# A join of two transfer chains in a Mamba and MoE kernel: queued with both chains as inputs, its gate released by its due landing

## The chip, the core and the metric

The program runs on one core of one Trainium2 chip. The metric is the device time of one execution in microseconds; the runs given are medians of several executions. A core has five queues that run in order by themselves and wait for each other through semaphores: PE (TensorE, matrix products into the PSUM banks), DVE (VectorE), ACT (ScalarE), POOL (GpSimd) and SP (SyncE, which here only issues transfers). POOL also issues transfers that add to what already lies at their target. An instruction that waits holds everything behind it in its own queue.

## The reference: what is computed

A "macaron" layer on 4 x 1024 tokens of 128 features: half a mixture of experts, a Mamba block, half a mixture of experts again, each with a layer norm in front and a residual around it.

```python
x = x + 0.5 * ffn(layernorm(x), ...)
x = x + attn(layernorm(x), ...)          # the Mamba block
x = x + 0.5 * ffn(layernorm(x), ...)

# ffn: 8 experts, every expert on every token, weighted
h = silu(x @ w_gate[e]) * (x @ w_up[e]); out += cw[e] * (h @ w_down[e])
# cw: product of two softmaxes over the experts (one at temperature 0.1), made to sum to one

# attn (Mamba, d_inner 256, 16 states)
xs, z = split(x @ W_in);  xc = silu(conv4(xs) + conv_b)
dbl = xc @ W_x;  dt = softplus(dbl[:, :64] @ W_dt + b_dt);  B, C = dbl[:, 64:80], dbl[:, 80:96]
h[t, :, n] = exp(dt * A[:, n]) * h[t-1, :, n] + dt * xc * B[t, n]
y[t] = sum over n of h[t, :, n] * C[t, n]  +  xc * D
out = (y * silu(z)) @ W_out
```

The sum over the 16 states n is the part that this change touches.

## The kernel before

**Tiling and stages.** The 4096 tokens are 8 blocks of 512. Each block goes through three stages: first mixture (kind 1), Mamba (m0 to m7), second mixture (kind 2). The 16 mixture stages run one after the other and make up the main loop; `order` lists them: kind 1 for blocks 0 to 3, then both kinds in turn. A mixture stage is 16 "halves" of two 128-wide slices each: six products into the PSUM tile `pg` (`gate_part`), a Silu on ACT into `h` (L536), six products into `pu` (`up_part`), `h * pu` on DVE (L561), and the down products of an earlier half into `pd` (L614). `pg` and `pu` have one buffer each, so the `pu` products of a half can't start before the L561 of the half before has read `pu`. On the finished `pd` of an expert ACT copies it to `tmp` (L636), and POOL multiplies it by the expert's weights and adds it to `acc` (L645, L648).

**The Mamba work rides along.** While one block's mixture runs on PE, the Mamba stage of another is fed in between as events. A block's 16 states take, per state n: `exp(dt*A)` on ACT (L892), on DVE the product with B (L906, `prod`), two scans (L918, `step`) and the product with C, either on DVE (L964) or "aside" on POOL (L954). The result of state n then has to be summed. `gather` does that by adding transfers that POOL issues: even n into `y`, odd n into the tile of state 1, called `odd`; so there are two chains, (k, 0) and (k, 1), each in order within itself. After state 15 a last transfer, the **join** (L938), adds `odd` to `y`. Then the **gate** multiplies `y` by silu(z): on DVE in blocks 0 and 7 (L986, `quick`), on POOL in the others (L991). Then PE does the output projection (`outproj`, tile `po`, L1002) and DVE adds it to x (L1009).

**Who sets the order.** The schedule is written out by hand: the order of the calls is the order of the instructions of each queue. A planner, `Plan`, keeps a modelled clock for each engine (`plan.pe`, `plan.dve`, `plan.act`, `plan.pool`), adds the cost given to each piece of work, and puts off work whose inputs aren't due. `plan.hi` and `plan.lo` hold pending DVE work; `lo` holds the states' products and scans. `fill` puts them into DVE's queue while they fit by the model before the next L561.

POOL has its own list, `pend`. `pool_put` appends an item: [function, cost, ready time, done, due time, chain, lane]. If `plan.lo` is empty it runs the whole list at once; otherwise items are run after each state's `prod` (`pool_run`) or by `pool_flush`. `pool_next` takes, of the first item of each chain, the one that can start earliest; `pool_start` gives that time: the ready time, `plan.pool`, and for a transfer the landing of the chain's last transfer, which its lane holds. A transfer is modelled to land YDMA = 5.9 after its issue.

**The join and gate before.** `gather` puts the join into chain (k, 0) with a ready time of the later of its data and the odd lane's landing, plus YDMA. When the join is run, its function first runs what is left of chain (k, 1) (L936, L937). The gate is an event of the list `back` at slot EPI + v + GT; its condition holds as soon as the join has been put into the list, that is once `scanned` exists. The gate then calls `pool_need`, which runs chain (k, 0) up to and with the join. Events that are held are forced after 12 slots (WAIT).

**Other work named later.** `dtfin` makes `dx` for the next Mamba block, on POOL (L881) in blocks 1 to 7; its states' first product L906 needs it. `cw1` to `cw3` make a mixture's weights by turns on POOL (L448, L454, L460) and DVE (L446, L453, L459); `cwt` transposes them on PE (L469). `zproj` (L975) makes z. The PSUM bank `misc` is shared by all the small products, among them `zproj`, `cwt` and `outproj`.

Of the kernel before, what the change touches and what calls it, by code (L numbers as in the profile page):

```python
# [25 lines left out]
EPI = 130  # L26
# [6 lines left out]
GT = 4  # L33
# [12 lines left out]
NEVER = 1e9  # L46
WAIT = 12
LOAD = 3.0
YDMA = 5.9
# [124 lines left out]
def tile_macaron_mamba_moe(  # L174
# [25 lines left out]
    NS = A_log.shape[1]  # L200
# [379 lines left out]
    def down(s, c):  # L580
# [41 lines left out]
        def weigh():  # L622
            cwb = d.pop(("cwb", e))
            d["tail"] = True
            plan.dve = max(plan.dve, pool_need(d["sum"]))
            tmp = sb.tile([P, TB], F32, tag="tmp", bufs=TMP, name=f"tmp_{kind}_{k}_{e}")
            V.tensor_tensor(tmp, pd, cwb, ALU.mult)
            V.tensor_tensor(d["acc"], d["acc"], tmp, ALU.add)
            plan.dve += 0.6
# [38 lines left out]
    def ffn_end(s):  # L668
        kind, k = order[s]
        d = ffn.pop(s)  # L670
        if "take" in d:
            plan.act_need(d["take"])
        plan.need(lambda: not d.get("tmp") or d["tmp"][3])
        at = d["tmp"][4] if "tmp" in d else pool_need(d["sum"])
        pt = misc(f"fo_{kind}_{k}")
        for j in range(J):
            T.transpose(pt[:, j * P : (j + 1) * P], d["acc"][:, j * P : (j + 1) * P], ident)
        x = xt[k]

        def upd():  # L680
            V.tensor_tensor(x, x, pt.rearrange("p (j h) -> p j h", j=J), ALU.add)
            fed.add(k)
            if kind == 2:
                nc.sync.dma_start(
                    out=of[k * TB : (k + 1) * TB, :].rearrange("(j p) h -> p j h", p=P), in_=x
                )

        plan.reader = plan.put(upd, 0.6, plan.on_pe(0.44, at))
# [15 lines left out]
    pend, credit = [], [0.0]  # L704

    def pool_put(fn, cost, ready, chain="w", dma=None):
        it = [fn, cost, ready, False, None, chain, dma]
        pend.append(it)
        if not plan.lo:
            pool_run(None)  # L710
        return it

    def pool_start(it):
        at = max(it[2], plan.pool)
        if it[6] is not None:
            at = max(at, it[6].get("landed", 0.0))
        return at

    def pool_next():
        heads, seen = [], set()  # L720
        for it in pend:
            if it[5] not in seen:
                seen.add(it[5])
                heads.append(it)
        return min(heads, key=pool_start) if heads else None

    def pool_run(after):
        credit[0] = min(credit[0] + CAP, CAP)
        while pend and (after is None or credit[0] > 0.0):
            it = pool_next()  # L730
            if after is not None and it[6] is not None and pool_start(it) > max(plan.pool, plan.dve) + AHEAD:
                break
            pool_one(after, it)

    def pool_one(after, it):
        pend.remove(it)
        ins = it[0]()
        it[3] = True
        if it[6] is not None:
            plan.pool = pool_start(it) + it[1]  # L740
            it[4] = it[6]["landed"] = plan.pool - it[1] + YDMA
            return
        credit[0] -= it[1]
        it[4] = plan.on_pool(it[1], max(it[2], plan.dve))
        if after is not None:
            tc.add_manual_dep(
                ins.ins, after.ins.name, mybir.DependencyInfo(mybir.DependencyClass.Sync, mybir.DependencyReason.DATA),
                reason="shared SBUF port",
            )

    def pool_flush():
        while pend:
            it = pool_next()
            if it[6] is None or pool_start(it) > max(plan.pool, plan.pe - 1.0):
                return
            pool_one(None, it)

    def pool_need(it):
        if it not in pend:
            plan.need(lambda: it[3])  # L760
        while not it[3]:
            pool_one(None, next(o for o in pend if o[5] == it[5]))
        return it[4]


    def mamba_events(k):
        d = {}
# [120 lines left out]
        def exps(n):  # L888
            plan.need_lo(4 * OUT)
            da = d["da", n] = big(f"da_{nm}_{n}")  # L890
            for i in range(ND):
                S.activation(da[:, i, :], d["dt"][:, i, :], AF.Exp, scale=A_sb[:, i, n : n + 1])  # L892
            t = plan.on_act(1.22, 0.0, "exp")
            if n == 0:
                if fast:
                    plan.need(lambda: d["dx_it"][3])
                else:
                    t = max(t, pool_need(d["dx_it"]))
            for f, cost in ((prod, 1.21), (lambda n: step(n, 0), 1.2), (lambda n: step(n, 1), 1.2), (read, 1.2)):
                it = plan.put(lambda f=f: f(n), cost, t, low=True)  # L900
            d["read", n] = it
# [21 lines left out]
        lane = [{}, {}]  # L923

        def gather(n, da, at):
            q = n % 2
            if n == 1:
                d["odd"] = da
            else:
                to = d["odd"] if q else d["y"]  # L930
                it = pool_put(lambda: G.dma_start(out=to, in_=da, accum_op=ALU.add), 0.9, at, (k, q), lane[q])
            if n < NS - 1:
                return

            def join():
                while any(o[5] == (k, 1) for o in pend):  # L936
                    pool_one(None, next(o for o in pend if o[5] == (k, 1)))  # L937
                return G.dma_start(out=d["y"], in_=d.pop("odd"), accum_op=ALU.add)  # L938

            ready = max(at, lane[1].get("landed", 0.0)) + YDMA  # L940
            d["scanned"] = pool_put(join, 0.9, ready, (k, 0), lane[0])

        def read(n):
            hb = d.pop("hb")
            da = d.pop(("da", n))
            bcb = d.pop(("bcb", n))
            d.pop(("read", n))
            plan.act_need(*d["y_it"])
            if d["aside"]:
                if not last:  # L950
                    V.tensor_reduce(st_sb[:, :, n : n + 1], da[:, :, TB - 1 : TB], AX.X, ALU.max)

                def weigh():
                    ins = G.tensor_tensor(da, da, bcb[:, 1:2, :].to_broadcast([P, ND, TB]), ALU.mult)  # L954
                    ahead["free"] += 1
                    pump()
                    return ins

                pool_put(weigh, 2.4, plan.dve, (k, n % 2))
                gather(n, da, plan.dve + 2.5)  # L960
                return
            if not last:
                V.tensor_copy(st_sb[:, :, n : n + 1], hb[:, :, TB - 1 : TB])
            V.tensor_tensor(da, hb, bcb[:, 1:2, :].to_broadcast([P, ND, TB]), ALU.mult)  # L964
            ahead["free"] += 1
            pump()
            gather(n, da, plan.dve + 0.1)

        def zproj(i):
                if i == 0:  # L970
                    d["zs"] = big(f"zs_{nm}")
                zs = d["zs"]
                d["zp"] = i + 1
                pz = misc(f"z{i}_{nm}")
                T.matmul(pz, w_in_sb[:, DI + i * P : DI + (i + 1) * P], d["xT"], start=True, stop=True)  # L975
                S.activation(zs[:, i, :], pz, AF.Silu)
                plan.bank = plan.on_act(0.6, plan.on_pe(0.86), "silu")
# [41 lines left out]
        v = w + LATE[k]  # L1019
# [31 lines left out]
        for q in range(NS // 2):  # L1051
# [8 lines left out]
        back = [  # L1060
            (EPI + v, lambda: zproj(0), free),
            (EPI + v + 2, lambda: zproj(1), free),
            (EPI + v + GT, gate, lambda: 0.0 if "scanned" in d else NEVER),
            (EPI + v + PO + (0 if quick else POW), outproj, lambda: max(free(), gated_at())),
        ]

        def gated_at():
            return (d["gated"][4] if d["gated"][3] else NEVER) if "gated" in d else NEVER
# [3 lines left out]
    chains = []  # L1072
# [19 lines left out]
    for s in range(len(order)):  # L1092
        add(8 * GPS * s, ffn_events(s))
        kind, k = order[s]
# [3 lines left out]
    for k in range(NBLK):  # L1098
        front, mid, back = mamba_events(k)
        add(START[k], front)  # L1100
        add(START[k], mid, 99)
        add(START[k], back)
# [62 lines left out]
```

## Time and profile before

| what | value |
|---|---|
| three runs | 1292.55, 1292.98, 1295.13 us; median 1292.98 |
| the profiled execution, its own time | 1294.15 us |
| its span, first to last instruction | 1292.4 us |
| matmuls on PE, DVE, ACT, POOL instructions | 4728, 1253, 1171, 624 |
| adding transfers from POOL into `y` and into `odd` | 72 and 56, 512 KB each |
| median from issue to landing of these | 9.1 and 9.5 us |
| the join, issue to landing, least, median, largest of 8 | 4.4, 4.5, 5.3 us |
| mean granted TensorE clock | 0.997 |

A line of a timeline reads: start in us, duration in us, engine, source line, operation, output<-inputs, how many were merged, and in brackets the idle time of that engine just before and what ended it. A line of the table of waits reads: engine, tile and line that waited, what it waited for, total us, times, longest us. A line of the table by stretches gives, for a stretch of time, the busy time of each engine with its number of instructions, the granted TensorE clock as a share of full speed, and the load of the transfers. Where the releaser is named "issue" the profile shows nothing that was waited for; a wait for several things is put down to the last that the profile saw, which can name the wrong one.

### The profile page before, as it was taken

Reading aid. Unit: us, or ns where it says so; the run is one execution under the profiler, and the core shown is the slowest. Engines: PE = TensorE matmul, PEld = TensorE weight load, DVE = VectorE, ACT = ScalarE, POOL = GpSimd, SP = SyncE. Lnnn points to the kernel's source line nnn. Section 1 sums busy time; section 2 is a strip of 40 time slices with the busy share of each in tenths; the row PEclk is TensorE's granted clock in tenths of the full one; section 3 lists DMA queues with packets and bytes.
Section 4 is the critical chain, followed back from the end, with each engine's and each line's share of the span. In section 5 each row is a group of like instructions: output and inputs, shape, how many; then the busy total and the mean of one; then the engine's idle time right before and its main releaser. Section 6 shows DMA issues by size and latency. Waiting matters only on the chain.

```text
span 1292.4 us, 14294 instructions
## 1 busy us (share of the span) xinstructions
PE 1257.2 (97%) x4728; PEld 853.9 (66%) x4728; DVE 1050.8 (81%) x1253; ACT 901.5 (70%) x1171; POOL 660.3 (51%) x624
## 2 busy tenths in 40 slices
PE   7999999989999999999999999999999999999998
PEld 5776665656666666666666666666666666668885
DVE  5875599978895899889769998997698889957675
ACT  5775766857867769767667786676777787646663
POOL 1012364637565647575467576554566657543400
PEclk9999999999999999999999999999999999999999
DMA  3420368757675668786737787676377867751110
GB/s 120 140 64 25 84 165 193 172 149 159 135 178 143 163 152 173 173 178 157 187 89 184 164 203 177 142 190 143 82 176 156 208 144 183 184 116 49 33 35 24
DMA packets 90635, 180.65 MB, mean 140 GB/s; under 512 B 9408, under 2 KB 22592, under 8 KB 90560
## 3 DMA queue, kind: packets, MB, share of 16 engines
q1 hardware_dynamic: 72128, 112.61, 31.8%
q0 software_dynamic: 18432, 67.12, 26.5%
q8 instruction: 37, 0.61, 0.2%
q14 instruction: 38, 0.31, 0.1%
HBM read 109.71 MB, written 2.88 MB: 87 GB/s over the span
## 4 chain that ended last, share of the span: by engine, by line
PE 73%; DMA 6%; DVE 4%; ACT 4%; issue 3%; POOL 3%; SPq 0%; POOLq 0%; DVEq 0%; ACTq 0%
PE pd L614 21%; PE pu L545 7%; PE pg L545 7%; PE pu L547 7%; PE pu L546 7%; PE pg L547 7%; PE pg L546 7%; DMA bcb_m<-bc_m 3%; PE pd L600 2%; DMA da_m<-da_m 2%; PE pd L608 1%; DMA y_m<-da_m 1%; DVE h L561 1%; PE xs_m L798 1%; ACT da_m L892 1%
## 5 line engine op out<-in xcount | busy, mean ns | idle before, releaser
L561 DVE TENSOR_TENSOR h<-h,pu 128x1024 f32<-128x1024 f32 x256 | 311.1, 1215 | 176.0 <-PE pu L547 124.4
L614 PE MATMUL pd<-h,wd 128*128 128x512 f32 x848 | 403.7, 592 | 1.4 <-ACT acc L636 0.7
L536 ACT ACTIVATE h<-pg 128x1024 f32<-128x1024 f32 x256 | 262.5, 1026 | 160.1 <-PE pg L547 156.5
L545 PE MATMUL pg<-xh_f,wh 128*128 128x512 f32 x512 | 272.5, 532 | 2.3 <-ACT h L536 1.4
L645 POOL TENSOR_TENSOR tmp<-tmp,cwb 128x512 f32<-128x512 f32 x98 | 137.1, 1399 | 208.6 <-ACT tmp L636 76.6
L614 PEld LDWEIGHTS pd<-h,wd 128*128 128x128 f32 x848 | 158.0, 189 | 114.3 <-issue 93.4
L545 PE MATMUL pu<-xh_f,wh 128*128 128x512 f32 x512 | 211.7, 414 | 3.1 <-DVE h L561 2.9
L547 PE MATMUL pg<-xh_f,wl 128*128 128x512 f32 x512 | 202.7, 396 | 0.0
L546 PE MATMUL pu<-xl_f,wh 128*128 128x512 f32 x512 | 202.4, 395 | 0.0
L546 PE MATMUL pg<-xl_f,wh 128*128 128x512 f32 x512 | 202.3, 395 | 0.0
L547 PE MATMUL pu<-xh_f,wl 128*128 128x512 f32 x512 | 202.1, 395 | 0.0
L954 POOL TENSOR_TENSOR da_m<-da_m,bcb_m 128x1024 f32<-128x1024 f32 x67 | 161.5, 2411 | 47.0 <-DVE hb_m L906 47.0
L906 DVE TENSOR_TENSOR hb_m<-dx_m,bcb_m 128x1024 f32<-128x1024 f32 x128 | 169.9, 1327 | 11.1 <-DMA bcb_m<-bc_m 8.1
L892 ACT ACTIVATE da_m<-dt_m,A_sb 128x512 f32<-128x512 f32 x256 | 163.9, 711 | 0.6
L545 PEld LDWEIGHTS pg<-xh_f,wh 128*128 128x128 f32 x512 | 96.7, 189 | 68.6 <-issue 30.9
L648 POOL TENSOR_TENSOR acc<-acc,tmp 128x512 f32<-128x512 f32 x98 | 137.1, 1399 | 7.7
L546 PEld LDWEIGHTS pg<-xl_f,wh 128*128 128x128 f32 x512 | 97.1, 190 | 52.3 <-issue 38.7
L545 PEld LDWEIGHTS pu<-xh_f,wh 128*128 128x128 f32 x512 | 96.7, 189 | 32.7 <-DVE h L561 7.6
L546 PEld LDWEIGHTS pu<-xl_f,wh 128*128 128x128 f32 x512 | 96.7, 189 | 24.8 <-issue 4.1
L547 PEld LDWEIGHTS pu<-xh_f,wl 128*128 128x128 f32 x512 | 96.7, 189 | 22.6
L547 PEld LDWEIGHTS pg<-xh_f,wl 128*128 128x128 f32 x512 | 96.5, 189 | 22.6
L636 ACT COPY tmp<-pd 128x512 f32<-128x512 f32 x111 | 64.7, 583 | 66.6 <-PE pd L614 55.1
(137 smaller groups left out, 1649.1 us busy)
## 6 DMA issues: line engine op xcount, KB each, us to landing
bcb_m<-bc_m SPq DMA_DIRECT2D x128, 512.0 KB
y_m<-da_m POOLq DMA_DIRECT2D x72, 512.0 KB, 9.1
cwb<-cd_f SPq DMA_DIRECT2D x128, 256.0 KB
da_m<-da_m POOLq DMA_DIRECT2D x56, 512.0 KB, 9.5
x<-in_L_attn_x_dram SPq DMA_DIRECT2D x8, 256.0 KB
wraw<-in_L_ffn_w_gate_dram SPq DMA_DIRECT2D x8, 256.0 KB
wraw<-in_L_ffn_w_up_dram SPq DMA_DIRECT2D x8, 256.0 KB
wd<-in_L_ffn_w_down_dram SPq DMA_DIRECT2D x8, 256.0 KB
```

Of the source, the lines that this page charges most:

```text
L536: S.activation(h, pg, AF.Silu)
L545: T.matmul(o[:, q, :], wh[e][:, i, cols], d["xh"], start=True, stop=False)
L546: T.matmul(o[:, q, :], wh[e][:, i, cols], d["xl"], start=False, stop=False)
L547: T.matmul(o[:, q, :], wl[e][:, i, cols], d["xh"], start=False, stop=True)
L561: V.tensor_tensor(h, h, pu, ALU.mult)
L614: T.matmul(d["pd"], wd[e][:, cols], h[0], start=(f == 0), stop=(f == FC - 1))
L636: S.copy(t, pd)
L645: it = put(lambda: G_.tensor_tensor(t, t, cwb, ALU.mult), 1.25, at)
L648: it = put(lambda: G_.tensor_tensor(acc, acc, t, ALU.add), 1.25, at)
L892: S.activation(da[:, i, :], d["dt"][:, i, :], AF.Exp, scale=A_sb[:, i, n : n + 1])
L906: mul = V.tensor_tensor(hb, d["dx"], bcb[:, 0:1, :].to_broadcast([P, ND, TB]), ALU.mult)
L954: ins = G.tensor_tensor(da, da, bcb[:, 1:2, :].to_broadcast([P, ND, TB]), ALU.mult)
```

## The change

- The join is put into the list as soon as state 15 has been put, with its data's time as its ready time. After the `pool_put` two entries are appended to the item: the odd chain and the odd lane.
- An item with these two entries is a candidate only when no earlier item of either chain is left, and starts, by the model, not before the landing in either lane. `pool_need` runs items of both chains until it is done. The loop in the join's function is gone.
- The gate's event holds until the join has been run and its due landing (`[4]`) has come by the planner's clock of PE.
- No instruction and no transfer of the computation is added or removed.

```diff
@@ pool_start
         if it[6] is not None:
             at = max(at, it[6].get("landed", 0.0))
+        if len(it) > 7:
+            at = max(at, it[8].get("landed", 0.0))
         return at
@@ pool_next
         for it in pend:
-            if it[5] not in seen:
-                seen.add(it[5])
+            if it[5] not in seen and (len(it) < 8 or it[7] not in seen):
                 heads.append(it)
+            seen.add(it[5])
@@ pool_need
         while not it[3]:
-            pool_one(None, next(o for o in pend if o[5] == it[5]))
+            chains = it[5:6] + it[7:8]
+            pool_one(None, next(o for o in pend if o[5] in chains))
@@ gather
-            if n < NS - 1:
-                return
-
+            if n == NS - 1:
+                tie(at)
+
+        def tie(at):
             def join():
-                while any(o[5] == (k, 1) for o in pend):
-                    pool_one(None, next(o for o in pend if o[5] == (k, 1)))
                 return G.dma_start(out=d["y"], in_=d.pop("odd"), accum_op=ALU.add)
 
-            ready = max(at, lane[1].get("landed", 0.0)) + YDMA
-            d["scanned"] = pool_put(join, 0.9, ready, (k, 0), lane[0])
+            d["scanned"] = pool_put(join, 0.9, at, (k, 0), lane[0])
+            d["scanned"].append((k, 1))
+            d["scanned"].append(lane[1])
@@ back
-            (EPI + v + GT, gate, lambda: 0.0 if "scanned" in d else NEVER),
+            (EPI + v + GT, gate, lambda: d["scanned"][4] if "scanned" in d and d["scanned"][3] else NEVER),
```

## The prediction

> **What bounds the kernel now.** I began with the page: PE works 97% of the span, and nothing else comes near.
>
> ```profile
> PE 1257.2 (97%) x4728; PEld 853.9 (66%) x4728; DVE 1050.8 (81%) x1253; ACT 901.5 (70%) x1171; POOL 660.3 (51%) x624
> ```
>
> So only what makes PE wait, or stop waiting, counts. Next the tables of waits of PE and of POOL:
>
> ```profile
> PE pt_f L361 <- ACT xn_f L351: 6.8, 1, 6.8
> PE po_m L1002 <- DVE x L681: 4.9, 1, 4.9
> ...
> PE z_m L975 <- DVE ex_f L421: 2.2, 1, 2.2
> ...
> PE cwt_f L469 <- DVE x L1009: 1.0, 1, 1.0
> ```
> ```profile
> POOL y_m L938 <- DMA da_m<-da_m: 68.2, 8, 11.2
> ```
>
> The eight joins hold POOL for 68.2 us, but PE pays in one place only, block 0's output projection, 4.9 us. The timelines of POOL, DVE and PE show how:
>
> ```profile
> 271.92 0.86 POOL L938 DMA_DIRECT2D y_m<-da_m  x1 [8.11 <-DMA da_m<-da_m]
> ```
> ```profile
> 276.49 1.23 DVE L986 TENSOR_TENSOR zs_m<-zs_m,y_m 128x1024 f32<-128x1024 f32 x1 [7.24 <-DMA y_m<-da_m]
> ```
> ```profile
> 278.37 3.66 PE L1002 MATMUL po_m<-w_out_sb,zs_m 128*128 128x128 f32 x16 [4.94 <-DVE x L681]
> ```
>
> The join goes out at 271.92 and has landed at 276.4; DVE's gate stands at the head of its queue from 269.25, and PE's projection waits for the gate (the releaser named, L681, is only the next DVE row). In blocks 1 to 7 the projection starts 1.5 to 5.8 us after its gate has ended: those gates cost PE nothing.
>
> **What the change moves.** It adds and removes no instruction of the computation, so I compared the order of each queue in the two built programs. PE's order is nearly the same: only block 0's projection moves, behind one more `pg` and `pu`, and some small products move by up to three halves. The new condition on the gate's event thus moves a projection in block 0 alone. On POOL the join still stands directly behind the last odd transfer in blocks 0, 1, 3, 5, 6 and 7; in 2 and 4 one L645/L648 pair slips in front. POOL's waits at the joins therefore stay. What moves is DVE's order, around block 0's gate and behind the joins of blocks 1, 3, 5 and 6.
>
> The reason for the second lies in the code. If `plan.lo` is empty when the join is put, `pool_put` runs it at once, before the two entries are appended. Counted while the program is built, it is empty in blocks 1, 3, 5, 6 and 7. The item is then an ordinary one of the even chain: its modelled start ignores the odd landing. Before, the model put that start at the odd transfer's landing + 5.9, so 11.8 us after its issue; the trace has 10.8, 12.0, 9.9, 7.6 and 5.2 us (blocks 1, 3, 5, 6, 7). Now the model lets POOL go on about ten us too soon, and `fill` puts DVE work that needs POOL's next results in front of L561. DVE will stand there, and PE behind it.
>
> **Block 0, a gain.** Now a scan, L681, L964, L906, a scan and L561 stand before the gate on DVE: 1.28 + 0.68 + 1.23 + 1.23 + 1.22 + 1.20 = 6.8 us from 269.25, so L561 ends at 276.0, the gate (landing 276.4) at 277.7. On PE `pg` of the next half ends at 275.5, its `pu` waits for that L561 until 276.05 and ends at 277.45, the projection takes 1.8 (its usual row) from 277.7, four down products 1.72: the half after begins at 281.25. It begins at 286.82 now. Gain 5.5 us; 4.9 if a row is late, 5.9 if all fit. Part of this is the clock, in the table by stretches:
>
> ```profile
> 273.50:278.30 4.80, 0.00 (x0) 0.00 (x0) 1.81 (x3) 0.61 (x1) 3.73 (x3) 1.00 0.60 130
> 278.40:281.70 3.30, 3.30 (x15) 3.30 (x16) 3.23 (x3) 0.00 (x0) 0.00 (x0) 0.50 0.76 188
> ```
>
> After 4.9 us without a matmul PE ran 3.4 us at half clock, 1.7 us lost. [...] The row shows full clock through 4.8 us of idleness, and I go by the row.
>
> **Block 1, a loss.** The rows of now:
>
> ```profile
> 397.95 0.86 POOL L938 DMA_DIRECT2D y_m<-da_m  x1 [9.89 <-DMA da_m<-da_m]
> 398.51 2.71 POOL L881 TENSOR_TENSOR dx_m<-dt_m,xc_m 128x1024 f32<-128x1024 f32 x1
> ...
> 403.76 1.23 POOL L448 TENSOR_TENSOR cw_f<-ex_f 128x32 f32<-128x32 f32 x1
> ```
> ```profile
> 401.93 1.22 DVE L561 TENSOR_TENSOR h<-h,pu 128x1024 f32<-128x1024 f32 x1 [4.57 <-ACT h L536]
> 403.06 1.82 DVE L906 TENSOR_TENSOR hb_m<-dx_m,bcb_m 128x1024 f32<-128x1024 f32 x1
> ...
> 407.74 0.18 DVE L453 TENSOR_REDUCE cs_f<-cw_f 128x4 f32<-128x32 f32 x1
> ```
> ```profile
> 404.95 0.40 PE L545 MATMUL pu<-xh_f,wh 128*128 128x512 f32 x1
> ```
>
> Now DVE does L561, then L906, L561, L453. In the changed order L906, L453, a scan, L459 and a scan stand before that first L561. L906 can't start before `dx` at 401.25 and takes 1.82; L453 needs L448, which with DVE out of its way ends at 404.0 to 404.4 (0.25 to 0.65 us); then 0.18, 1.21, 0.17, 1.21 and L561 1.22: it ends near 408.2 instead of 403.15. PE's next `pu`, at 404.95 now, waits until 408.25: 3.3 us (3.1 to 3.5). Two halves on, DVE has 6.2 us of work before an L561 while PE's half takes 4.5, another 0.9 (0 to 1). Together 4.2. Behind DVE's L906 wait nothing but PE's `pu` is held; the POOL gate, moved behind L460 and an L954 (2.4 us), keeps over 2 us to its projection.
>
> **Block 3, the same order.** Join at 651.48, `dx` done at 654.75, L906 1.91, L448 done at 657.6 to 658.4; L561 ends at 661.5 to 662.4. PE's `pu` is at 657.05 now: 4.5 to 5.4, I take 5.0, and 0.9 later. This stall is as long as block 0's, so half clock, 1.7 (0 if it falls short). Together 7.6.
>
> **Block 5.** L453 now comes two L561 later than in the changed order:
>
> ```profile
> 907.75 0.87 POOL L938 DMA_DIRECT2D y_m<-da_m  x1 [9.02 <-DMA da_m<-da_m]
> 908.31 0.59 POOL L448 TENSOR_TENSOR cw_f<-ex_f 128x32 f32<-128x32 f32 x1
> ```
> ```profile
> 902.68 1.22 DVE L561 TENSOR_TENSOR h<-h,pu 128x1024 f32<-128x1024 f32 x1 [3.08 <-PE pu L547]
> ```
>
> L453 waits for L448 until 908.7, L561 ends at 910.0 instead of 903.9, and `pu`, at 905.97 now, loses 4.1 (3.9 to 4.3). `cwt` moves up three halves on PE, to 914.0 on the delayed clock, while L460 comes at 915.2, behind `dx` (914.3), L455 and L459: 1.2; its old wait of 1.0 goes. Together 4.3.
>
> **Block 6.** `dx` moves behind the join. The odd transfer can leave some 6 us sooner (1026.6 for 1032.6), the join 7.6 to 11 after it, `dx` 3 us later: L906, at 1035.30 now, starts between 1036 and 1039.3. Its L561 then ends at 1041 to 1044.3, with `pu` due at 1043.22; with DVE's queue full behind it 0 to 3.3, I take 1.0. **Block 7** has nothing urgent behind its join. **Block 4:** `shift` (L420, L421), which frees the bank that `zproj` waits 2.2 us for, stands before an L906 of 3.99 us instead of behind it: gain 2.2 (0 to 2.4).
>
> **Sum.** -5.5 - 2.2 + 4.2 + 7.6 + 4.3 + 1.0 = +9.4 us. The profiled span goes from 1292.4 to 1301.8; its execution was 1294.15, 1.75 more than its span and 1.2 above the median of the runs. From the median 1292.98 I predict **1302.4 us**.
>
> **Rivals.**
> - *Faster: the joins come early enough.* Were the odd transfers to land as in block 7, 5.2 us after issue, the joins of 1, 3 and 5 would go out 5 to 7 us sooner, DVE would not wait, and the gains of 7.7 alone stay: 1285.3. It decides from about 3.3 us sooner in block 1. Block 7's row speaks for it; seven of eight rows of 7.6 to 12.0 us speak against it.
> - *No change.* The joins stay where they were, so the change does not do what it says in most blocks; if DVE's new waits fell into its idle time there (4.57 us before L561 in block 1, 3.08 in block 5), only half of the stalls would reach PE: +17.1 halved, -7.7: 1293.8. Against it: PE's `pu` starts only 1.8 to 2.1 us after the L561 that moves by 5 to 7.
> - *Slower still.* Half clock after the stalls of blocks 1 and 5 too, 3.4, and block 6 at its upper end, 2.3: 1308.1. The 3.3 and 4.1 us of idleness, under the 4.9 seen, speak against it.
>
> **How the numbers follow.** My forecast has 0.72 (its own range 1297 to 1306), faster 0.06, no change 0.08, slower still 0.14. The low bounds (3.1 + 4.5 + 4.1 + 0 - 5.9 - 2.4) give +3.4 or 1296.4, the upper ones (4.5 + 8.1 + 4.5 + 3.3 - 4.9 - 0) +15.5 or 1308.5; a little beyond on either side for the neighbouring cases, 1295.5 to 1309, is the range. A difference within 0.2%, 2.6 us, can't be told from none here: faster 0.06, same 0.07, slower 0.87.
>
> **What would show it.** Right: no wait of PE at `po` in block 0 and no stretch of half clock there; L906 or L453 as DVE rows with 3 to 5 us of idle time before them, released by POOL, right behind the joins of blocks 1, 3 and 5, and PE's `pu` waiting for L561 there; POOL's wait at L938 still near 68. Wrong: those DVE rows without idle time; joins that land sooner; a PE wait at a projection in blocks 1 to 7; or new waits far from the joins, which would mean that DVE's order, not the joins, sets the time.

## Result and profile after

| | before | after |
|---|---|---|
| median (lowest to highest) | 1293.06 us (1292.55 to 1295.13, 4 runs) | 1315.0 us (1311.56 to 1316.61, 4 runs) |
| ratio, 95% interval | | 1.0163 [1.0137, 1.0189] |
| profiled execution, its span | 1294.15, 1292.4 us | 1316.61, 1314.8 us |
| granted TensorE clock, mean | 0.997 | 0.990 |

The change costs 21.9 us. The forecast was 1302.4 (1295.5 to 1309.0): slower, but by less than half. The first line of the profile after, busy time of each engine:

```profile
PE 1267.6 (96%) x4728; PEld 857.4 (65%) x4728; DVE 1057.6 (80%) x1255; ACT 901.6 (69%) x1171; POOL 655.0 (50%) x622
```

PE has the same 4728 products and is busy 10.4 us longer: that is not a wait, the products themselves took longer. The other half are waits. From the tables of waits of PE, DVE and POOL, after:

```profile
PE pu L545 <- DVE h L561: 19.2, 9, 5.2
...
PE cwt_f L469 <- POOL cw_f L460: 2.3, 1, 2.3
```
```profile
DVE cs_f L453 <- POOL cw_f L448: 12.7, 3, 10.0
DVE hb_m L909 <- POOL dx_m L884: 12.2, 4, 5.7
...
POOL y_m L940 <- DMA da_m<-da_m: 44.5, 6, 11.5
```

The wait of 4.9 us at `po` is gone, and 19.2 us at `pu` are new. Behind them DVE stands for POOL's L448 and L884, which stand behind the join. (The operations behind the change sit two or three lines lower than before: L906 is L909, L881 is L884, L938 is L940, L986 is L989, L1002 is L1005.)

PE's order is almost the same in both programs, so the start of `pu` in half n can be set beside that of half n before, and the growth of the difference between two halves is what that stretch lost. The table gives it for the two profiled executions (22.5 us in all) beside the terms of the sum:

| stretch, halves | what lies in it | measured, us | forecast, us |
|---|---|---|---|
| 50 to 60 | block 0's join, gate, projection | -0.2 | -5.5 |
| 60 to 74 | `lt` of a router, no join | +1.9 | 0 |
| 74 to 82 | behind block 1's join | +3.9 | +4.2 |
| 120 to 136 | block 3 | +8.3 | +7.6 |
| 145 to 160 | block 4 | -3.0 | -2.2 |
| 175 to 186 | block 5 | +6.5 | +4.3 |
| 186 to 212 | block 6 | +3.0 | +1.0 |
| 223 to 232 | block 7, `cwt` | +2.4 | 0 |
| the rest | | -0.3 | 0 |

**Block 3** went as worked out. Timelines of POOL, DVE and PE, after:

```profile
658.03 0.86 POOL L940 DMA_DIRECT2D y_m<-da_m  x1 [11.54 <-DMA da_m<-da_m]
658.60 2.68 POOL L884 TENSOR_TENSOR dx_m<-dt_m,xc_m 128x1024 f32<-128x1024 f32 x1
```
```profile
661.31 2.29 DVE L909 TENSOR_TENSOR hb_m<-dx_m,bcb_m 128x1024 f32<-128x1024 f32 x1 [5.67 <-POOL dx_m L884]
664.97 0.19 DVE L453 TENSOR_REDUCE cs_f<-cw_f 128x4 f32<-128x32 f32 x1 [1.36 <-POOL cw_f L448]
...
667.37 1.20 DVE L561 TENSOR_TENSOR h<-h,pu 128x1024 f32<-128x1024 f32 x1
```
```profile
668.62 0.80 PE L545 MATMUL pu<-xh_f,wh 128*128 128x512 f32 x1 [5.22 <-DVE h L561]
```

POOL stands 11.5 us at the join; `dx` comes behind it; DVE, whose order now has L909 and L453 ahead of the L561, stands 5.67 and 1.36 us; PE stands 5.22 us for that L561. (Waits in this text are the idle times in brackets.)

**Block 0** did not. Timelines of POOL, DVE and PE, after:

```profile
271.63 0.86 POOL L940 DMA_DIRECT2D y_m<-da_m  x1 [7.55 <-DVE x L681]
272.19 1.60 POOL L645 TENSOR_TENSOR acc<-acc,cwb 128x512 f32<-128x512 f32 x1
273.43 2.69 POOL L957 TENSOR_TENSOR da_m<-da_m,bcb_m 128x1024 f32<-128x1024 f32 x1
```
```profile
272.46 4.76 DVE L909 TENSOR_TENSOR hb_m<-dx_m,bcb_m 128x1024 f32<-128x1024 f32 x1
277.31 1.28 DVE L921 TENSOR_TENSOR_SCAN da_m<-da_m,st_sb,hb_m 128x512 f32<-128x512 f32 x1
278.50 1.20 DVE L561 TENSOR_TENSOR h<-h,pu 128x1024 f32<-128x1024 f32 x1
279.62 1.22 DVE L989 TENSOR_TENSOR zs_m<-zs_m,y_m 128x1024 f32<-128x1024 f32 x1
```
```profile
279.76 0.80 PE L545 MATMUL pu<-xh_f,wh 128*128 128x512 f32 x1 [3.79 <-DVE h L561]
```

The gate no longer waits for the transfer, but L909 took 4.76 us instead of 1.23: it ended at 277.22, 1.1 us after the second of POOL's products. So L561 ended at 279.7 instead of 276.0, and the wait only moved from `po` to `pu`.

**The clock.** The table by stretches, after, in steps of 3.4 us around three waits (time, length, then busy time of PE, PEld, DVE, ACT, POOL, the granted clock, transfers): block 0, block 5, block 1.

```profile
275.00:278.40 3.40, 0.97 (x5) 0.45 (x3) 3.31 (x2) 1.08 (x2) 1.98 (x2) 1.00 0.36 86
278.40:281.80 3.40, 2.04 (x5) 1.66 (x6) 3.40 (x4) 0.00 (x0) 0.00 (x0) 0.50 0.78 158
281.80:285.20 3.40, 3.40 (x16) 3.21 (x15) 1.45 (x2) 0.00 (x0) 0.00 (x0) 0.50 1.03 254
```
```profile
916.70:920.10 3.40, 0.85 (x2) 0.02 (x1) 0.00 (x0) 1.72 (x3) 0.68 (x2) 1.00 0.16 30
920.10:923.50 3.40, 1.53 (x4) 1.24 (x5) 1.31 (x2) 0.00 (x0) 3.24 (x6) 0.50 0.80 154
923.50:926.90 3.40, 3.40 (x7) 1.92 (x6) 1.40 (x2) 0.00 (x0) 3.00 (x5) 0.50 0.00 0
```
```profile
404.70:408.10 3.40, 2.30 (x9) 1.21 (x7) 2.06 (x4) 2.12 (x4) 2.31 (x7) 1.00 0.29 74
408.10:411.50 3.40, 1.80 (x7) 1.43 (x8) 3.37 (x5) 3.39 (x5) 0.42 (x1) 1.00 0.00 0
411.50:414.90 3.40, 3.40 (x13) 2.20 (x12) 3.37 (x5) 2.11 (x3) 3.32 (x3) 1.00 0.00 0
```

The stretches with PE busy 0.97 and 0.85 of 3.4 us were followed by half clock, which went on for a second stretch; PE had stood for 1.4 and 1.9 us of the first. Block 1's wait, 2.70 us, lies across two stretches, with 1.1 us without a product in the one and 1.6 in the other, and brought none. Half clock before the last product lasted 3.4 us before and 23.9 us after (6.8, 3.4, 6.8 and 6.8 us), with PE busy in 3.4 and 19.5 us of it. I take half of that busy time as lost, an estimate: 1.7 and 9.8 us, so 8.1 us more. (In block 0, after, the products of `pu` start 0.43 us apart at half clock, from 280.35 on, and 0.23 apart at full clock, from 288.67 on.)

### The profile page after: what moved, and what is told of

The parts are those of the page before. It is cut to its first block, busy times and chain, and to the rows that moved or that the text cites. A ratio compares the mean times of both kernels' runs of the same rounds, so it can differ in the third digit from the quotient of the medians.

```text
span 1314.8 us, 14288 instructions
## 1 busy us (share of the span) xinstructions
PE 1267.6 (96%) x4728; PEld 857.4 (65%) x4728; DVE 1057.6 (80%) x1255; ACT 901.6 (69%) x1171; POOL 655.0 (50%) x622
## 5 line engine op out<-in xcount | busy, mean ns | idle before, releaser
L561 DVE TENSOR_TENSOR h<-h,pu 128x1024 f32<-128x1024 f32 x256 | 310.9, 1214 | 172.2 <-PE pu L547 137.1
L645 POOL TENSOR_TENSOR tmp<-tmp,cwb 128x512 f32<-128x512 f32 x98 | 136.5, 1393 | 245.2 <-ACT tmp L636 102.6
L545 PE MATMUL pu<-xh_f,wh 128*128 128x512 f32 x512 | 214.6, 419 | 19.8 <-DVE h L561 19.2
L909 DVE TENSOR_TENSOR hb_m<-dx_m,bcb_m 128x1024 f32<-128x1024 f32 x128 | 172.9, 1351 | 18.6 <-POOL dx_m L884 12.2
L957 POOL TENSOR_TENSOR da_m<-da_m,bcb_m 128x1024 f32<-128x1024 f32 x65 | 155.6, 2394 | 43.2 <-DVE hb_m L909 43.2
L648 POOL TENSOR_TENSOR acc<-acc,tmp 128x512 f32<-128x512 f32 x98 | 135.3, 1381 | 7.7
```

The source lines that it names most:

```text
L545: T.matmul(o[:, q, :], wh[e][:, i, cols], d["xh"], start=True, stop=False)
L561: V.tensor_tensor(h, h, pu, ALU.mult)
L645: it = put(lambda: G_.tensor_tensor(t, t, cwb, ALU.mult), 1.25, at)
L648: it = put(lambda: G_.tensor_tensor(acc, acc, t, ALU.add), 1.25, at)
L909: mul = V.tensor_tensor(hb, d["dx"], bcb[:, 0:1, :].to_broadcast([P, ND, TB]), ALU.mult)
```

## Experiments

Each time stands beside runs of the kernel before on the same chip (medians 1294.60, 1294.43 and 1293.14 us in the three groups).

### The two parts of the change

First the join alone, with the gate's old condition:

```diff
-            (EPI + v + GT, gate, lambda: d["scanned"][4] if "scanned" in d and d["scanned"][3] else NEVER),
+            (EPI + v + GT, gate, lambda: 0.0 if "scanned" in d else NEVER),
```

> The join queued as in the changed kernel, the gate's event with its old condition. Early planner clock (my theory): in blocks 1 to 7 DVE's order is that of the changed kernel, so PE's stalls at pu behind the joins of blocks 1, 3 and 5 stay at about 2.9, 5.4 and 4.6 us, and the wait of 2.5 us at cwt in block 7 too; block 0's gate goes back to its old place, where PE waits some 4 to 5 us at po instead of 4 us at pu: 1311 to 1318. Rival (the new condition of the gate's event costs the time, by moving gates and projections): without it the time falls back to 1292 to 1296.

1312.14 us, ratio 1.0131 [1.0107, 1.0155]; PE's waits at `pu` 3.4, 4.3 and 3.5 us, at `cwt` 2.3. Most of the loss, 17.5 of 21.9 us, comes from how the join is queued. Then the condition alone, the same line changed in the kernel before:

> The kernel before with the new condition of the gate's event alone; the join is put and run as before. Early planner clock: the join's model keeps 11.8 us from the odd issue, so L906 and L453 keep their places among the L561 of blocks 1, 3, 5, 6 and 7, no stall of PE over 1.5 us is added there, and block 0 stays as it is: 1288 to 1296. Rival (the condition costs the time): 1305 or more.

1297.21 us, ratio 1.0017 [1.0006, 1.0029]: 1.2 us above the range given, but no cause of 21.9 us. It adds a wait of 1.4 us at `pu` in half 141, far from a join.

### How late the model thinks the join is

The item gets its second chain and lane before it can be run, so that the model never starts the join ahead of the odd landing:

```diff
-    def pool_put(fn, cost, ready, chain="w", dma=None):
-        it = [fn, cost, ready, False, None, chain, dma]
+    def pool_put(fn, cost, ready, chain="w", dma=None, *more):
+        it = [fn, cost, ready, False, None, chain, dma, *more]
...
-            d["scanned"] = pool_put(join, 0.9, at, (k, 0), lane[0])
-            d["scanned"].append((k, 1))
-            d["scanned"].append(lane[1])
+            d["scanned"] = pool_put(join, 0.9, at, (k, 0), lane[0], (k, 1), lane[1])
```

> The changed kernel, but the item carries the odd chain and its lane from the start, so the model of the join's start is never without the odd landing (issue + 5.9 us). The program's order changes only a little: L453 goes one half later in blocks 1 and 5, L906 stays where it is in the changed kernel. Early planner clock: 5.9 us is still some 4 to 6 us less than the trace has between odd issue and join, so DVE still stands at L906 in blocks 1 and 3; block 5's stall of 4.6 us, which L453 makes, falls by one half's work to 0 to 2: 1306 to 1314. Rival (the empty list alone makes the loss, 5.9 us would do): 1286 to 1294.

1303.85 us, ratio 1.0072 [1.0049, 1.0095]: under the range. Waits of DVE and PE:

```profile
DVE hb_m L909 <- POOL dx_m L884: 11.1, 4, 4.6
...
DVE cs_f L453 <- POOL cw_f L448: 4.9, 1, 4.9
```
```profile
PE pu L545 <- DVE h L561: 9.0, 8, 3.6
...
PE cwt_f L469 <- POOL cw_f L460: 3.4, 1, 3.4
```

L909 still stands 11.1 us; L453 falls from 12.7 to 4.9, and PE's waits at `pu` from 19.2 to 9.0, of which 3.6 are block 0's. DVE's wait for `dx` stays, as expected, but PE's longest wait behind it is 1.9 us (block 3), and no half clock follows. Then as much delay as the model had before the change:

```diff
         if len(it) > 7:
-            at = max(at, it[8].get("landed", 0.0))
+            at = max(at, it[8].get("landed", 0.0) + YDMA)
```

> As the one before, and the join's modelled start is the odd landing + 5.9 us, as in the kernel before (11.8 us after the odd issue). DVE's order in blocks 1, 3, 5, 6 and 7 is nearly that of the kernel before; block 0's gate stands two L561 later than before. Early planner clock: the stalls at pu behind the joins of blocks 1, 3, 5 and the wait at cwt in block 7 go (each under 1 us), the half clock behind them too; block 0 loses its wait at po of 4.9 us and the 3.4 us of half clock and gains 4 to 6: 1285 to 1291. Rival (other moves of DVE's order and the projections cost the time): 1300 or more. Rival (block 0's gain is always eaten by POOL's products beside L906): 1290 to 1295.

1294.62 us, ratio 1.0001 [0.9990, 1.0011]. In blocks 1, 3, 5, 6 and 7 the planner's own numbers have the join 0.9 to 2.5 us behind the odd issue in the changed kernel, 5.9 in the run before this one and 11.8 here, as in the kernel before; the loss is 21.9, 9.3 and 0 us. In blocks 0, 2 and 4 it is the kernel before whose model is early, 2.7, 3.7 and 0.9 us, because there the ready time is set while the last odd transfer is still in the list; the change makes it 6.2 to 6.6. Waits of DVE and PE:

```profile
DVE zs_m L987 <- DMA y_m<-da_m: 4.4, 1, 4.4
```
```profile
PE pu L545 <- DVE h L561: 4.1, 7, 1.4
PE po_m L1003 <- DVE zs_m L987: 3.9, 1, 3.9
```

No DVE row waits for `dx` or L448 among the larger ones, and no wait at `pu` is over 1.4 us. But the gain of 4 to 6 us in block 0 that I expected is not there, and not for the reason that the second rival gave, though the time lies in its range: L909 took 1.24 us. Here the products and another block's transfer go out ahead of the join, which lands 11.3 us after its issue at 271.4; the gate waits until 282.7.

### Blocks apart

A list `NEW` says in which blocks the change is made; the others keep the join, ready time and gate condition of before.

```diff
+                while k not in NEW and any(o[5] == (k, 1) for o in pend):
+                    pool_one(None, next(o for o in pend if o[5] == (k, 1)))
...
+            if k not in NEW:
+                ready = max(at, lane[1].get("landed", 0.0)) + YDMA
+                d["scanned"] = pool_put(join, 0.9, ready, (k, 0), lane[0])
+                return
...
+            (EPI + v + GT, gate, lambda: NEVER if "scanned" not in d else 0.0 if k not in NEW else d["scanned"][4] if d["scanned"][3] else NEVER),
```

`NEW = (0,)`:

> The change in block 0 alone; the joins and gates of the other blocks as in the kernel before. Theory (the gain of block 0 is eaten there: the join holds POOL until 271.6, the two products behind it, L645 and L957 in the changed kernel, then run beside the next L909, which stands until they are done): L909 takes 4 to 4.8 us instead of 1.23, PE waits some 4 us at pu instead of 4.9 at po, half clock for 3.4 to 6.8 us; no stall behind the joins of blocks 1, 3, 5: within 2 us of the kernel before run beside it. Rival (block 0's 5.5 us are gained, and lost elsewhere in the changed kernel): 4 to 6 us less than the kernel before.

1293.90 us, ratio 0.9995 [0.9980, 1.0009]; L909 (L910 here) took 4.98 us, PE waited 4.1 at `pu`, half clock 6.8 us there and 3.4 at 373.9. Then POOL's products go behind the next L909:

```diff
             pool_one(after, it)
+            if after is not None and len(it) > 7:
+                break
```

> As the one before, and POOL's products behind the join are released by the end of the next L909 product instead of the one before it. Theory: L909 takes 1.2 to 1.3 us again, the L561 behind it ends near 276, PE waits under 1 us at pu and at po, no half clock near 278: 4 to 6 us less than the kernel before. Rival (the join itself lands later than 277, or DVE's order is late anyway): PE waits 3 us or more at po or pu all the same, within 2 us of the kernel before.

1291.74 us, ratio 0.9970 [0.9956, 0.9984]: a gain, under the 4 to 6 us expected. DVE's timeline, this run, then the same with blocks 2 and 4 added (below):

```profile
273.68 1.23 DVE L912 TENSOR_TENSOR hb_m<-dx_m,bcb_m 128x1024 f32<-128x1024 f32 x1
...
281.45 1.23 DVE L998 TENSOR_TENSOR zs_m<-zs_m,y_m 128x1024 f32<-128x1024 f32 x1 [4.03 <-DMA y_m<-da_m]
```
```profile
271.79 1.23 DVE L912 TENSOR_TENSOR hb_m<-dx_m,bcb_m 128x1024 f32<-128x1024 f32 x1
...
276.44 1.44 DVE L998 TENSOR_TENSOR zs_m<-zs_m,y_m 128x1024 f32<-128x1024 f32 x1 [0.91 <-DMA y_m<-da_m]
```

L909's time falls from 4.98 to 1.23 in both: the products were the cause. Whether the 4 to 6 us are then had depends, in these two traces, on the join's landing. In the first it went out at 273.5 and the gate found it landed at 281.4; in the second at 270.9 and 276.4. So the rival's condition came true in the first, whose PE waits 3.6 us at `po`; in the second it waits there no more. The runs of the first lie between 1287.69 and 1295.03. What sets the landing is left open.

`NEW = (0, 2, 4)`, where the list is not empty, without and with the products put off:

> The change in blocks 0, 2 and 4, where the list of DVE's states is not empty when the join is put, so that the item gets both chains before it is run; blocks 1, 3, 5, 6, 7 as in the kernel before. Theory (only the joins run at once with an unfinished item cost time): no stall over 1.5 us behind a join but block 0's; block 0 about nil, block 4 gains the 2 to 3.4 us that it gained in the changed kernel: 1 to 4 us less than the kernel before. Rival (the late planner clocks of the other blocks were what moved block 4): within 1 us of the kernel before.

> As the one before, with POOL's products behind these three joins released by the next L909. Theory: block 0's 4 to 6 us and block 4's 2 to 3.4 us are both had: 6 to 9 us less than the kernel before. Rival (products put off by one L909 come late for the sums of the experts or for dx, or hit the next gate): less than 3 us gained, with a new wait of PE in stages 3 to 9.

1290.78 us, ratio 0.9964 [0.9952, 0.9977], and 1287.60 us, ratio 0.9950 [0.9937, 0.9963]. Both times are as the theory said; the second is faster than both kernels, by 6.8 and some 27 us. It has one longer wait that the theory did not name: 3.0 us for `lt` at 367.7, 1.6 before, with 3.4 us of half clock behind it.

`NEW = (1, 3, 5, 6, 7)`, where the list is empty:

> The complement of the run with blocks 0, 2 and 4: the change in blocks 1, 3, 5, 6 and 7 alone, where the list of DVE's states is empty when the join is put. Theory (only these blocks cost time): everything that the changed kernel lost and what blocks 0, 2, 4 gave back, 22 to 27 us more than the kernel before run beside it, with the stalls of PE at pu of 2.5 to 5.5 us behind the joins of 1, 3 and 5 and the wait of 2.5 us at cwt in block 7. Rival (the parts act on each other, a stall of one absorbs that of another): 12 to 20 us more.

1317.67 us, ratio 1.0186 [1.0169, 1.0203], 24.5 us more. Waits of PE:

```profile
PE pu L546 <- DVE h L562: 14.3, 8, 4.6
...
PE cwt_f L470 <- POOL cw_f L461: 2.3, 1, 2.3
```

With the -3.7 us of blocks 0, 2 and 4 that makes 20.8, against 21.9 measured, whose interval goes from 17.7 to 24.4: the parts add up within it.

### What a wait of PE costs beyond itself

```diff
+HOLD = {229: 5, 233: 6, 237: 7, 241: 8, 245: 9, 249: 10}
...
         def mul():
+            for _ in range(HOLD.get(g // 2, 0)):
+                V.tensor_scalar(h, h, 1.0, None, ALU.mult)
             V.tensor_tensor(h, h, pu, ALU.mult)
```

> The kernel before with DVE held up in the last two stages, ahead of the L561 of six halves (229, 233, 237, 241, 245, 249), by 5, 6, 7, 8, 9 and 10 products of h with 1.0: PE's waits at pu grow from one to the next. With 0.65 to 1.2 us for a product and some 4.5 us that DVE and PE have to spare there, the waits are 0 to 1.5 us for the first and 2 to 7.5 us for the last. Theory (the clock is set for stretches of 3.41 us on a grid; a stretch at full clock in which PE stood about 2 us or more is followed by one at half clock, one at half clock in which it stood about 1.2 us or more by another): waits under 1.9 us bring no half clock, waits of 2 to 3.8 us sometimes, all longer ones 3.4 or 6.8 us of it, and each 3.4 us of it costs 0.8 to 1.7 us on top of the wait. Rival (the prediction's reading of the row of block 0): no half clock after waits under 4.8 us, and 3.4 us of it after longer ones.

1334.04 us, ratio 1.0312 [1.0297, 1.0328]. PE's waits at `pu`, these six and four short ones:

```profile
PE pu L546 <- DVE h L564: 32.2, 10, 6.2
```

The six were 4.4, 2.2, 6.2, 6.1, 4.9 and 5.8 us: they do not grow evenly, since the products with 1.0 did not (five took 5.5 us at the first wait, six 4.3 at the second). All but the second were followed by 6.8 us of half clock, the second by none; the mean granted clock of this run was 0.984. The stretches at the second and third wait:

```profile
1194.40:1197.80 3.40, 1.84 (x9) 1.16 (x7) 3.19 (x5) 0.00 (x0) 0.00 (x0) 1.00 0.00 0
1197.80:1201.20 3.40, 2.77 (x14) 2.05 (x14) 0.88 (x2) 2.79 (x4) 1.18 (x1) 1.00 0.00 0
...
1214.90:1218.30 3.40, 1.09 (x5) 0.56 (x3) 3.30 (x4) 2.52 (x3) 1.64 (x2) 1.00 0.00 0
1218.30:1221.70 3.40, 0.00 (x0) 0.00 (x0) 3.23 (x4) 0.00 (x0) 1.88 (x2) 0.51 0.00 0
1221.70:1225.10 3.40, 2.92 (x7) 2.35 (x8) 0.55 (x2) 1.57 (x2) 0.40 (x2) 0.50 0.00 0
```

From half 223 on this kernel loses 41.3 us to the one before; its six waits sum to 29.6. The other 11.7 are near the same estimate, half of PE's busy time in the five times of half clock: (5.1 + 3.0 + 5.7 + 4.7 + 3.7) / 2 = 11.1. The rival's reading, nothing under 4.8 us, falls with the first wait, 4.4.

## Why the prediction was right in direction and too small

- **The early clock of the list that is empty: right.** The model of POOL ran ahead, DVE's order put L909 and L453 in front of an L561, and PE waited: undone by the model's delay alone, and confined to blocks 1, 3, 5, 6 and 7 by the runs with the blocks apart. The waits without the clock's part were forecast at 4.2, 5.9 and 4.3 us in blocks 1, 3 and 5. After has 3.9, 8.3 - 2.9 = 5.4 and 6.5 - 2.5 = 4.0 (half of PE's 5.7 and 4.9 us busy at half clock taken off).
- **The price of the half clock: the step that failed.** "The row shows full clock through 4.8 us of idleness, and I go by the row." The row gave the clock during the idle time; in both traces the half clock came in the stretch behind it (from 278.35 us before, from 278.38, 373.95, 667.50 and 920.09 after). The sum had 1.7 us gone in block 0 and 1.7 come in block 3, nothing net. By the estimate above the runs had 8.1 us more, of them 1.7 at 374 us, where a wait of 1.6 us for `lt` had become one of 2.0. This is over half of the 13.1 us between forecast and the two traces (22.5 - 9.4). One stretch of half clock for a stall was too few as well: the trace has two behind the waits of 3.79, 4.42 and 5.22 us, and one behind that of 2.00. Block 1's wait of 2.70 us had none behind it; it lay across two stretches, 1.1 us in one and 1.6 in the next; I had not worked that out.
- **Block 0's gain: the second step that failed.** "1.28 + 0.68 + 1.23 + 1.23 + 1.22 + 1.20 = 6.8 us": the first product on DVE after the join took 4.76, not 1.23, and the half clock that I had going grew from 3.4 to 6.8 us. -0.2 instead of -5.5; 2.7 of these 5.3 us are the clock's and stand in the 8.1 already. The trace of before had shown the like: an L906 of 3.99 us beside POOL's L954, which I used in block 4 and did not look for in block 0.
- **Block 7, "nothing urgent behind its join": wrong, 2.4 us.** POOL's L460 is behind it, and `cwt`, moved up 1.5 halves, waits 2.3 us for it.
- **Blocks 4 and 6:** the mechanism of 4 as said, 2.4 us for 2.2; the rest of its 3.0 is a wait of 1.4 us at `pu` ahead of the join that went. 6 cost 3.0, within my 0 to 3.3, where I took 1.0, but not where I had put it: `dx` came late as forecast and the `pu` that I named was met; half of the 3.0 is a wait of 1.5 us at `pu` two halves on.
- **Rivals.** "Faster" and "no change" fell: the join went out 6.9 to 12.4 us after the odd issue in seven blocks, 10.0, 12.4 and 10.6 in blocks 1, 3 and 5, and the waits at `pu` reached PE almost whole. "Slower still", half clock behind the stalls of blocks 1 and 5 too, was the right mechanism, though block 1 paid none in this trace; priced at one stretch of 3.4 us each, its 1308.1 is still 7 us short. "POOL's wait at L938 still near 68" was wrong in size (44.5 in six rows, and 7.5 of block 0 put down to another releaser), since the products put in front of the joins of blocks 2 and 4 fill it.

## What to carry to other kernels

A planner's clock that runs ahead of a queue costs nothing on that queue; it costs where another engine's fixed order is laid out by it, so after a change in what an item waits for, check that the model still delays it in every case, the empty list too. Price a stall of the matrix engine with the half clock behind it; in these traces that went by the idle time inside each stretch of 3.413 us and not by the stall's length. The price is a range: in the trace after, by the estimate, nothing for a wait of 2.70 us, 1.7 us for one of 2.00 and 2.9 for one of 5.22. When a queue is held up, ask what runs beside its late work: here that ate the gain, a product of 4.76 us instead of 1.23.

## What the runs showed of the hardware

**Half clock in stretches of 3.413 us.** Ahead of the last product half clock went from 278.35 to 281.76 us before, and from 278.38 to 285.21, 373.95 to 377.37, 667.50 to 674.33 and 920.09 to 926.91 us after. In each of these two traces the borders lie a whole number of 3.413 us apart, to a thousandth of a stretch. I cut both traces by that grid, between 25 us and 1270 us, and took PE's idle time in each stretch that has a next one there. At full clock, 2.41, 2.54, 3.41 and 3.41 us idle were followed by half clock, 1.91 us too (after), 1.98 us not (before), and none of the 712 stretches with 1.63 us or less. At half clock, 1.12, 1.38 and 1.88 us idle were followed by more of it, 0.01 us or less by full clock, five times. The rows of the run with growing waits have 2.31 us idle with half clock behind it, 1.56 us with none. What a wait cost beyond itself depended on where it fell: in the changed kernel, 2.70 us cost nothing and 2.00 us cost 1.7, by the estimate. Counted from the first instruction, the grid's first border lies at 1.87 us before and 1.90 after; the half clock of two other runs gives 2.8 (the model of before, granted clock 0.84 between 280 and 284 us) and 3.2 (growing waits, 0.51 between 1218.30 and 1221.70). So the trace before did not tell where a wait would fall in those two.

**DVE's products beside POOL's.** L909 took 4.76, 4.98 and 5.05 us in three kernels (the changed one, block 0 alone, blocks 0, 2 and 4) beside two products of POOL (L645 and L957 in the changed kernel), each time ending 1.1 us after the second of them, and 1.23 in the two runs where they were moved. Elsewhere it ended behind the first of two. In block 3 of the changed kernel L909 ended at 663.60, 1.1 us after L645, and the L648 behind, which needs the result of L645, took 2.14 us instead of 1.28. In the kernel before an L906 ended 1.1 us after L648, and the L954 behind, which does not need the result of L648, took 3.38 us instead of 2.4:

```profile
742.17 1.61 DVE L906 TENSOR_TENSOR hb_m<-dx_m,bcb_m 128x1024 f32<-128x1024 f32 x1
```
```profile
741.42 1.27 POOL L648 TENSOR_TENSOR acc<-acc,tmp 128x512 f32<-128x512 f32 x1
742.64 3.38 POOL L954 TENSOR_TENSOR da_m<-da_m,bcb_m 128x1024 f32<-128x1024 f32 x1
```

Which of the two happens, and why, these runs do not show.
